# A two-layer graph network on one core: layer 1's decaying weights by byte additions in runs of eight nodes instead of by matmuls over every block

## The chip, the cores and the metric

The kernel runs on one core of a Trainium2 chip. The metric is the device time of one launch in microseconds. Before the change it was 696.75 us, the median of three runs (694.16, 696.75 and 701.30). A profile of one execution shows the engines: PE (TensorE matmuls, with PEld for its weight loads), DVE (VectorE), ACT (ScalarE), POOL (GpSimd), SP (SyncE, which here only issues transfers), and the queues of transfers (DMA).

## What is computed

There are 4096 nodes with 64 features, and a 0/1 adjacency matrix of 4096 x 4096 with about 8 ones in a row (67 MB in float32, the one large input).

```
h = relu(layernorm(x))
# layer 0: a weighted mean over the neighbours of a hyperbolic distance direction
w = adj / max(rowsum(adj), 1e-8)
agg = einsum('ij,ijc->ic', w, logmap(h_i, h_j))
x = x + expmap(0, agg @ W0 + b0)
h = relu(layernorm(x))
# layer 1: neighbours weighted by powers of a half, by their rank in the row
support = h @ W1
rank = cumsum(adj != 0, axis=1);  deg = rank[:, -1];  k = min(deg, 100)
w = (adj != 0) * where(rank - (deg - k) > 0, 0.5 ** (deg - rank), 0)
x = x + w @ support + b1
```

So in layer 1 the last neighbour of a row weighs 1, the one before it 1/2, and so on. In the kernel every degree is at most 30, else a second, dense path (not executed here) takes over.

## The kernel before

**Load.** The adjacency is read in 32 blocks of 128 rows. One call `load(rb, n)` (L789) issues two transfers of 256 KB on SP's queue into two of four buffers `a_sb`, transposes eight 128 x 128 pieces on PE against the identity (L799, the adjacency piece is the stationary operand) into the PSUM tile `a_ps`, and copies them with one ACT instruction (L801) as fp8 into `masks[q]`: partitions are columns of the adjacency (neighbours), the free dimension holds the rows. There are 128 such calls; `pack` (L808) follows each with eight small matmuls that pack 16 columns into one number.

**Lists.** For every second row block DVE searches the packed words for the largest entries (`search`, L835) and turns them into indices of neighbours (`ell_lists`, L849: the first eight words of a row). What does not fit goes through `tail_split`, `tail_first` and `tail_second` into short lists per quadrant of eight row blocks.

**Layer 0, by gathers.** There are 16 units of two row blocks. POOL fetches the neighbours' rows of the table `tab_d` (260 bytes each) with one indirect transfer per list slot (`gather`, L987 to L1000): 320 in all, 16 to 22 in a unit, into one of two buffers `g`. For the units that have tail entries POOL also makes a one-hot `oh` (`tail_rows`, L1012), which PE transposes (L1017), ACT copies (L1019) and PE multiplies (L1023, result `sel`). Then come `differ` (L1036 to L1058: DVE differences, ACT square), `weigh` (L1070 to L1089: from L1070 on, the buffer `g` is free again) and `total` (L1100 to L1119). When a group of row blocks has all its units, `middle` (L1144) makes layer 0's output, the layernorm and layer 1's `support`, which `split` (L1202) writes as three bf16 parts `sup`; it borrows two of the `a_sb` buffers.

**Layer 1, the powers.** `ranks(p, n, j)` (L1215) goes through the 32 column blocks j from the last to the first, for each of 4 quadrants p of 1024 rows and its two halves n of 512. A running tile `t` in PSUM counts the neighbours behind each column: one matmul with `rest` adds what block j+1 still lacked (L1221), one with `before` (lower triangular, with -128 on the diagonal) gives block j (L1225); then one ACT instruction writes 2^-(t) as fp8 over the mask, one block higher (L1229), so that a column without an edge becomes zero. PE and ACT take turns here: each step of PE needs the ACT result of the step before. That is 504 matmuls and 256 ACT instructions.

**Layer 1, the sum.** `collect(c, p, n)` (L1238) multiplies those weights with `sup` for four groups of column blocks `sums` (16, 8, 6 and 2 blocks), 1024 matmuls (L1244), and adds the three parts to `acc` on DVE (L1252, L1256): 64 such pairs. `write` stores `acc`.

**Order.** Every call gets a due time in `plan` by hand (`at`, L1267), and a scheduler at build time lays out one fixed order for every engine from these. At run time each engine goes through its own order and waits where an operand is late. So an instruction of `differ` can sit on PE, ACT or DVE behind a `load`, `ranks` or `collect` that comes first in that engine's order. SP's order is: x, 32 transfers of the adjacency, `tab_d` (L760), 12 more, `hp_d` (L767), and then the rest with the lists' small transfers in between.

Of the kernel before, what the change touches and what calls it, by code (L numbers as in the profile page):

```python
# [11 lines left out]
F32 = mybir.dt.float32  # L12
BF16 = mybir.dt.bfloat16
# [6 lines left out]
P = 128  # L20
# [19 lines left out]
BIG = 128.0  # L40
# [4 lines left out]
F8W = mybir.dt.float8e5  # L45

# [5 lines left out]
EXTRA = 8  # L52
TAILW = CAND - ELL + EXTRA
# [6 lines left out]
W8_SHIFT = 15  # L60
# [478 lines left out]
def kernel(  # L539
# [33 lines left out]
    UC = 512  # L573
    NU = N // UC
# [6 lines left out]
    x_v = x.rearrange("(b p) c -> p b c", p=P)  # L581
    out_v = out.rearrange("(b p) c -> p b c", p=P)
# [8 lines left out]
    def by_rows(t):  # L591
        return t.rearrange("(b p) c -> p b c", p=P)

    with ExitStack() as fast:
# [5 lines left out]
        ident = const.tile([P, P], F32, name="ident")  # L600
# [7 lines left out]
        w_c = const.tile([P, 1], F32, name="w_c")  # L608
        nc.vector.memset(w_c, (W8_SHIFT - BIG) * LN2)
# [11 lines left out]
        rest = const.tile([P, P], BF16, name="rest_b")  # L621
# [4 lines left out]
        nc.vector.tensor_scalar(grp_i, part_i, 4, None, ALU.logical_shift_right)  # L626
# [7 lines left out]
        nc.vector.tensor_scalar(pw_i, part_i, GRP - 1, None, ALU.bitwise_and)  # L634
        nc.vector.tensor_scalar(pw_i, pw_i, 135, None, ALU.add)
# [81 lines left out]
        masks = [maskp.tile([P, NB + 1, QR], F8, name=f"mask{q}") for q in range(NQ)]  # L717

        adjp = fast.enter_context(tc.tile_pool(name="adjp", bufs=4))
        lst = fast.enter_context(tc.tile_pool(name="lst", bufs=1))  # L720

        prep = fast.enter_context(tc.tile_pool(name="prep", bufs=1))
        late2 = masks[NQ - 2].bitcast(F32).rearrange("p b c -> p (b c)")[:, 16 * QR // 4 :]
        gn_i = late2[0:1, 0:NG].bitcast(I32)
        nc.gpsimd.iota(gn_i, pattern=[[1, NG]], base=0, channel_multiplier=0)
# [6 lines left out]
        nc.vector.scalar_tensor_tensor(tri_f, ident, -BIG, tri_f, ALU.mult, ALU.add)  # L732
        nc.vector.tensor_copy(before, tri_f)
        nc.vector.tensor_scalar(rest, tri_f, -1.0, 1.0, ALU.mult, ALU.add)
# [7 lines left out]
        nc.sync.dma_start(out=xin, in_=x_v)  # L742
        tab = part(NB * D, DT)
        sq = part(NB * (D + DT), D)
        x2 = prep.tile([P, NB], F32, name="x2")
        ab = prep.tile([P, NB], F32, name="ab")
        sg = prep.tile([P, NB], F32, name="sg")
        h = tab[:, :, 1:DT]
        layernorm_relu(prep, xin, h, sq)
# [23 lines left out]
        mid = fast.enter_context(tc.tile_pool(name="mid", bufs=1))  # L773
        ps_a = fast.enter_context(tc.tile_pool(name="ps_a", bufs=2, space=PSUM))
        ps_w = fast.enter_context(tc.tile_pool(name="ps_w", bufs=1, space=PSUM))
        ps_t = fast.enter_context(tc.tile_pool(name="ps_t", bufs=2, space=PSUM))
# [9 lines left out]
        sums = [(0, 16, (0, 1)), (16, 8, (2,)), (24, 6, (3,)), (30, 2, (4,))]  # L786


        def load(rb, n):  # L789

            a_ps = ps_a.tile([P, 2, SB, P], BF16, name="a_ps")
            for m in range(2):
                a_sb = adjp.tile([P, UC], F32, name="a_sb")
                c = 2 * n + m
                nc.sync.dma_start(out=a_sb, in_=adj[bass.ts(rb, P), bass.ts(c, UC)])

                upper = a_sb.bitcast(BF16)[:, 1 : 2 * UC : 2]
                for k in range(SB):
                    nc.tensor.transpose(a_ps[:, m, k, :], upper[:, bass.ts(k, P)], ident_b)  # L799
            q, b = divmod(rb, QB)  # L800
            nc.scalar.activation(  # L801
                masks[q][:, 2 * SB * n : 2 * SB * n + 2 * SB, bass.ts(b, P)],
                a_ps.rearrange("p m k f -> p (m k) f"),
                AF.Copy,
                saturate=False,
            )

        def pack(rb, n):  # L808
# [12 lines left out]
            for j in range(2 * SB * n, 2 * SB * n + 2 * SB):  # L821
                nc.tensor.matmul(  # L822
                    words[:, rb % 2, bass.ts(j, GB)],
                    lhsT=masks[q][:, j, bass.ts(b, P)],
                    rhs=pk,
                    start=False,
                    stop=True,
                    skip_group_check=True,
                )
# [19 lines left out]
        def ell_lists(rb, nb):  # L849
# [9 lines left out]
            nc.vector.tensor_scalar(  # L859
                ci, ci, NG - 1, 4, ALU.bitwise_and, ALU.logical_shift_left  # L860
            )
            nc.vector.tensor_scalar(e, w.bitcast(I32), 23, None, ALU.logical_shift_right)
            nc.vector.tensor_scalar(kk, e, -134.0, None, ALU.add)
            nc.vector.tensor_tensor(t, kk, ci, ALU.add)
            nc.vector.scalar_tensor_tensor(ell_v[:, r2], kk, 0.0, t, ALU.is_gt, ALU.mult)
            nc.vector.tensor_scalar(ell_i[:, r2], ell_v[:, r2], -1.0, 0.0, ALU.add, ALU.max)

        def tail_split(q):
# [12 lines left out]
            nc.vector.tensor_scalar(  # L881
                gf, gf, NG - 1, 4, ALU.bitwise_and, ALU.logical_shift_left
            )
            kk = e.bitcast(F32)
            t = p.bitcast(F32)
            for n in range(3):
# [5 lines left out]
                nc.vector.tensor_scalar(kk, e, -134.0, None, ALU.add)  # L892
                nc.vector.tensor_tensor(t, kk, gf, ALU.add)
# [5 lines left out]
                    ALU.is_gt,  # L899
# [244 lines left out]
        def middle(m, stage):  # L1144
# [5 lines left out]
            if stage == 0:  # L1150
                st["hq", m], st["xq", m] = (
                    adjp.tile([P, UC], F32, name="a_sb") for _ in range(2)
                )
            ht = st["hq", m][0:D, :]
            hq, xq = (
                st[k, m][:, 0 : nb * D].rearrange("p (b c) -> p b c", b=nb)
                for k in ("hq", "xq")
            )
            if stage == 0:
                nc.sync.dma_start(out=hq, in_=by_rows(tab_d)[:, bs, 1:DT])  # L1160
                nc.sync.dma_start(out=xq, in_=x_v[:, bs, :])
# [34 lines left out]
            else:  # L1196
                c = [m in s[2] for s in sums].index(True)
                if m == sums[c][2][0]:
                    st["sup", c] = blk.tile([P, sums[c][1], 3 * D], BF16, name=f"sup{c % 2}")
                sup = st["sup", c][:, b0 - sums[c][0] : b0 - sums[c][0] + nb, :]  # L1200

                def split(gs, sp):  # L1202
                    res = xq[:, gs, :]
                    rest = sp
                    for n in range(3):
                        part = sup[:, gs, n * D : n * D + D]
                        nc.vector.tensor_copy(part, rest)
                        if n < 2:
                            nc.vector.tensor_tensor(res, rest, part, ALU.subtract)
                        rest = res  # L1210

                product(m, v, w1_sb, ht, split)


        def ranks(p, n, j):  # L1215

            if j == NB - 1:
                st["t", p, n] = ps_t.tile([P, SW], F32, name="t")
            t = st["t", p, n]
            if j < NB - 1:  # L1220
                nc.tensor.matmul(  # L1221
                    t, lhsT=rest, rhs=masks[p][:, j + 1, bass.ts(n, SW)],
                    start=False, stop=False, skip_group_check=True,
                )
            nc.tensor.matmul(  # L1225
                t, lhsT=before, rhs=masks[p][:, j, bass.ts(n, SW)],
                start=(j == NB - 1), stop=True, skip_group_check=True,
            )
            nc.scalar.activation(  # L1229
                masks[p].bitcast(F8W)[:, j + 1, bass.ts(n, SW)],  # L1230
                t,
                AF.Exp,
                bias=w_c,
                scale=-LN2,
                saturate=False,
            )

        def collect(c, p, n):  # L1238

            b0, nb, _ = sums[c]  # L1240
            o = ps_a.tile([P, 2, 3 * D], F32, name="a_ps")
            for k in range(2):
                for j in range(nb):
# [151 lines left out]
```

## Time and profile before

| What | Value |
|---|---|
| median of three runs | 696.75 us |
| the profiled execution, first to last instruction | 888.9 us (its time outside that span isn't given) |
| first indirect transfer of POOL starts | 57.60 us |
| last POOL instruction ends | 813.1 us |
| transfers | 89.19 MB, 85,590 packets, 46,098 of them under 512 B |
| adjacency loads by the chain of waits | 22% of the span |
| TensorE clock granted, mean | 0.719 of full speed |

The profiled execution is 28% longer than the median run. All durations below come from it. Its table of groups gives, for each line and engine, how often an instruction ran, the mean duration, and how long the engine stood idle just ahead of it; its chain of waits follows the last instruction back to what released it; its table of windows gives the busy time of the engines in a stretch.

### The profile page before, as it was taken

The numbers are of one execution on the slowest core, as the hardware profiler recorded it, in microseconds if no ns is written. First come the engines' busy times: TensorE is split into PE (matmuls) and PEld (weight loads), VectorE is DVE, ScalarE is ACT, GpSimd is POOL, SyncE is SP. The second block draws the span as 40 slices with busy tenths as digits, with TensorE's granted clock in tenths as the row PEclk, the third lists the DMA queues.
The fourth block names the chain that finished last, engine by engine and source line by source line (L and its number), as shares of the span: only waits on it lengthen the run. The fifth ranks groups of instructions, "written<-read, shape, count | busy, mean of one in ns | idle before, by whom it ended". The sixth has DMA issues, their size and how long they took to land.

```text
span 888.9 us, 11822 instructions
## 1 busy us (share of the span) xinstructions
PE 494.8 (56%) x4170; PEld 328.1 (37%) x4170; DVE 411.1 (46%) x1482; ACT 356.6 (40%) x550; POOL 368.3 (41%) x396
## 2 busy tenths in 40 slices
PE   3654245277115656725727828576568574367495
PEld 2421123144002423513415403323258473267383
DVE  4550144266101637305624638604644244739786
ACT  3543246286115745815907828365511011202100
POOL 0035752603771046172172262736574818751000
PEclk9995576677556957966956968869559595569585
DMA  7899446386235756735836510301121101210002
GB/s 212 238 165 145 92 136 168 94 245 196 49 71 154 218 133 159 233 76 166 265 67 190 146 24 18 49 12 31 23 46 18 24 16 24 31 23 4 0 2 51
DMA packets 85590, 89.19 MB, mean 100 GB/s; under 512 B 46098, under 2 KB 47634, under 8 KB 85522
## 3 DMA queue, kind: packets, MB, share of 16 engines
q1 hardware_dynamic: 66194, 74.93, 31.2%
q0 software_dynamic: 10240, 10.67, 9.2%
q10 hardware_dynamic: 9088, 2.75, 1.5%
q8 instruction: 34, 0.56, 0.3%
q14 instruction: 34, 0.28, 0.1%
HBM read 84.12 MB, written 4.19 MB: 99 GB/s over the span
## 4 chain that ended last, share of the span: by engine, by line
PE 27%; DMA 24%; issue 14%; DVE 13%; another core or an unknown queue 11%; POOL 5%; ACT 4%; SPq 1%; ACTq 0%; DVEq 0%; POOLq 0%
DMA a_sb<-in_adj 22%; PE a_ps L1244 7%; PE a_ps L799 6%; POOL g L995 4%; PE t L1225 4%; PE t L1221 4%; DVE red L1252 2%; ACT mask L1229 2%; PE sel L1105 2%; DVE d L1070 2%; PE words L1139 1%; PE words L822 1%; DMA mask<-in_x 1%; DVE acc L1256 1%
## 5 line engine op out<-in xcount | busy, mean ns | idle before, releaser
L995 POOL DMA_INDIRECT g<-tab_d,ell_i x256 | 257.4, 1005 | 368.5 <-DVE u L1071 102.0
L1229 ACT ACTIVATE mask<-t,w_c 128x512 fp8e5<-128x512 f32 x256 | 172.3, 691 | 149.5 <-remote 65.2
L799 PE MATMUL a_ps<-ident_b,a_sb 128*128 128x128 bf16 x1024 | 128.6, 263 | 120.6 <-DMA a_sb<-in_adj 91.0
L801 ACT ACTIVATE mask<-a_ps 128x1024 fp8e4<-128x1024 bf16 x128 | 131.4, 1027 | 135.5 <-remote 78.8
L1221 PE MATMUL t<-mask,rest_b 128*128 128x512 fp8e4 x248 | 115.6, 466 | 78.8 <-ACT mask L1229 51.1
L799 PEld LDWEIGHTS <-a_sb 128*128 128x128 bf16 x1024 | 80.5, 116 | 189.5 <-DMA a_sb<-in_adj 130.2
L1225 PE MATMUL t<-mask,before 128*128 128x512 fp8e4 x256 | 121.7, 476 | 4.6 <-ACT mask L1229 4.6
L1244 PE MATMUL a_ps<-sup,mask 128*128 128x192 bf16 x1024 | 110.0, 271 | 24.1 <-issue 12.5
L1244 PEld LDWEIGHTS <-mask 128*128 128x128 fp8e5 x1024 | 98.0, 108 | 34.0 <-issue 29.4
L822 PE MATMUL words<-pk,mask 128*128 128x8 bf16 x1024 | 48.4, 170 | 67.7 <-ACT mask L801 34.6
L822 PEld LDWEIGHTS <-mask 128*128 128x128 fp8e4 x1024 | 44.4, 104 | 105.3 <-issue 56.4
L843 DVE MAX8 cand<-wsb 128x8 f32<-128x256 f32 x96 | 36.0, 411 | 86.2 <-ACT wsb L833 66.5
L1012 POOL TENSOR_SCALAR oh<-row,tail_r 128x128 bf16<-128x128 bf16 x64 | 46.9, 747 | 56.8 <-DVE r L1111 33.1
L995 POOL DMA_INDIRECT g<-tab_d,tail_i x64 | 62.2, 972 | 18.8 <-issue 18.8
L1225 PEld LDWEIGHTS <-before 128*128 128x128 bf16 x256 | 28.0, 110 | 109.2 <-issue 106.9
L1252 DVE TENSOR_REDUCE red<-a_ps 128x128 f32<-128x384 f32 x64 | 35.6, 556 | 51.0 <-remote 26.4
L1019 ACT COPY mt<-mi 128x768 bf16<-128x768 bf16 (+1 forms) x12 | 8.7, 728 | 93.4 <-PE mi L1017 93.4
L1221 PEld LDWEIGHTS <-rest_b 128*128 128x128 bf16 x248 | 28.8, 116 | 20.3 <-issue 11.8
L1139 PE MATMUL words<-w_sb,a_sb 64*128 64x64 f32 x128 | 26.4, 366 | 13.2 <-issue 7.6
L1036 DVE TENSOR_TENSOR d<-g,hi 128x1024 f32<-128x1024 f32 x16 | 19.4, 1215 | 28.6 <-DMA a_sb<-in_adj 28.4
L1105 PE MATMUL sel<-d,mr 128*128 128x65 f32 x128 | 24.0, 346 | 14.5 <-DVE r L1111 6.2
L1070 DVE TENSOR_REDUCE d<-g 128x22 f32<-128x1408 f32 (+2 forms) x16 | 23.7, 1482 | 17.8 <-ACT g L1058 9.6
(285 smaller groups left out, 555.0 us busy)
## 6 DMA issues: line engine op xcount, KB each, us to landing
a_sb<-in_adj SPq DMA_DIRECT2D x256, 256.0 KB
g<-tab_d,ell_i POOLq DMA_INDIRECT x256
hp_d<-mask SPq DMA_DIRECT2D x1, 1560.0 KB
hr<-hp_d ACTq DMA_DIRECT2D x8, 146.2 KB
tab_d<-mask SPq DMA_DIRECT2D x1, 1040.0 KB
hi<-tab_d ACTq DMA_DIRECT2D x16, 64.0 KB
g<-tab_d,tail_i POOLq DMA_INDIRECT x64
out<-acc SPq DMA_DIRECT2D x8, 128.0 KB
```

Of the source, the lines that this page charges most:

```text
L799: nc.tensor.transpose(a_ps[:, m, k, :], upper[:, bass.ts(k, P)], ident_b)
L801: nc.scalar.activation(masks[q][:, 2 * SB * n : 2 * SB * n + 2 * SB, bass.ts(b, P)], a_ps.rearrange("p m k f -> p (m k) f"), AF.Copy, satu ...
L822: nc.tensor.matmul(words[:, rb % 2, bass.ts(j, GB)], lhsT=masks[q][:, j, bass.ts(b, P)], rhs=pk, start=False, stop=True, skip_group_check= ...
L995: nc.gpsimd.indirect_dma_start(out=g[:, k, :], out_offset=None, in_=tab_d, in_offset=bass.IndirectOffsetOnAxis(ap=i, axis=0),)
L1012: nc.gpsimd.tensor_scalar(oh[:, k, :], row128, row[:, k : k + 1], None, ALU.is_equal)
L1070: nc.vector.tensor_reduce(d2, u["g"][:, 0:ns, 1:DT], AX.X, ALU.add)
L1105: nc.tensor.matmul(ag[:, k // TB, :], lhsT=mr[:, k, :], rhs=d[:, E2 + k, :], start=(k % TB == 0), stop=(k % TB == TB - 1),)
L1221: nc.tensor.matmul(t, lhsT=rest, rhs=masks[p][:, j + 1, bass.ts(n, SW)], start=False, stop=False, skip_group_check=True,)
L1225: nc.tensor.matmul(t, lhsT=before, rhs=masks[p][:, j, bass.ts(n, SW)], start=(j == NB - 1), stop=True, skip_group_check=True,)
L1229: nc.scalar.activation(masks[p].bitcast(F8W)[:, j + 1, bass.ts(n, SW)], t, AF.Exp, bias=w_c, scale=-LN2, saturate=False,)
L1244: nc.tensor.matmul(o[:, k, :], lhsT=masks[p].bitcast(F8W)[:, b0 + j + 1, bass.ts(2 * n + k, P)], rhs=st["sup", c][:, j, :], start=(j == 0) ...
L1252: nc.vector.tensor_reduce(red, o.rearrange("p k (n c) -> p k c n", n=3), AX.X, ALU.add)
```

## The change

Nodes are renumbered: a partition now holds runs of eight neighbouring nodes (node = 1024 s + 8 p + l, with s a group of 1024 nodes, p the partition, l the place in the run) in place of nodes p apart by 128. So the eight column blocks of one s hold, on each partition, a run of eight consecutive columns. The transfers of x, of the table, of `hp_d` and of the output become contiguous per partition, and a load takes 1024 columns in one transfer of 512 KB, with three buffers of 4 KB per partition in place of four of 2 KB. The transposes read the adjacency with a stride of 32 bytes in place of 4.

The mask is stored as fp8 2^-14, whose byte is 4. `suffix(p, s)` adds bytes two at a time as int16 on DVE, so that each column of a run holds four times the count of edges at and behind it in the run; ACT then copies the run's total. `ranks(p, s)` counts over runs only, with `upto` and `before` (14 matmuls per quadrant in place of 126), ACT turns the result into a base byte per run, and one DVE instruction subtracts the eight columns' bytes from it. The byte is then read as fp8: its exponent is the power of two. As every column now has a value, edge or not, the sum over edges is done by parts: `middle` makes differences of `support` of neighbouring columns, over the runs with help of two small matmuls (`shift`, `carry`), and `collect` sums 33 blocks in five groups in place of 32 in four. `keep` copies `support` on ACT. The indices of the lists are made for the new numbers, with as many instructions.

In the built order POOL has the same 320 indirect transfers and 64 one-hots as before. `middle` takes one of the three `a_sb` buffers; in the built order of SP its first call now stands ahead of the last 22 of the 128 loads, where before all loads came first, and the searches of row blocks 24 to 31 stand on DVE behind units 8 and 9. The byte additions of a quadrant stand on DVE among the steps of `weigh`, `total` and `tail_split`.

```diff
-    x_v = x.rearrange("(b p) c -> p b c", p=P)
+    x_v = x.rearrange("(s p l) c -> p s l c", p=P, l=RUN)
+    adj_v = adj.rearrange("(s p l) c -> s l p c", p=P, l=RUN)
     def by_rows(t):
-        return t.rearrange("(b p) c -> p b c", p=P)
+        return t.rearrange("(p b) c -> p b c", p=P)
...
-        adjp = fast.enter_context(tc.tile_pool(name="adjp", bufs=4))
+        masks = [maskp.tile([P, NB, QR], F8W, name=f"mask{q}") for q in range(NQ)]
+        words16 = [m.bitcast(I16) for m in masks]
+        adjp = fast.enter_context(tc.tile_pool(name="adjp", bufs=3))
...
-        sums = [(0, 16, (0, 1)), (16, 8, (2,)), (24, 6, (3,)), (30, 2, (4,))]
+        sums = [range(0, 8), range(8, 16), range(16, 24), range(25, 30), (24, 30, 31, None)]
         def load(rb, n):
-            a_ps = ps_a.tile([P, 2, SB, P], BF16, name="a_ps")
-            for m in range(2):
-                a_sb = adjp.tile([P, UC], F32, name="a_sb")
-                c = 2 * n + m
-                nc.sync.dma_start(out=a_sb, in_=adj[bass.ts(rb, P), bass.ts(c, UC)])
...
+            a_sb = adjp.tile([P, UC], F32, name="a_sb")
+            nc.sync.dma_start(out=a_sb, in_=adj_v[rb // RUN, rb % RUN, :, bass.ts(n, UC)])
+            upper = a_sb.bitcast(BF16)[:, 1 : 2 * UC : 2].rearrange("p (f l) -> p l f", l=RUN)
+            a_ps = ps_a.tile([P, RUN, P], BF16, name="a_ps")
+            for l in range(RUN):
+                nc.tensor.transpose(a_ps[:, l, :], upper[:, l, :], ident_b)
...
+                def keep(gs, sp):
+                    nc.scalar.copy(v[:, gs, :], sp)
+                product(m, v, w1_sb, ht, keep)
...
+                    pv = ps_o.tile([P, SW], F32, name="o")[:, 0:D]
+                    nc.tensor.matmul(
+                        pv, lhsT=shift, rhs=st["y", s - 1][:, RUN - 1, 0:D], start=True, stop=(s == 1)
+                    )
...
+                    nc.vector.tensor_tensor(dd[:, 0, :], pv, v[:, 0, :], sub)
+                    nc.vector.tensor_tensor(dd[:, 1:n, :], v[:, 0 : n - 1, :], v[:, 1:n, :], sub)
...
+        def suffix(p, s):
+            w = words16[p][:, bass.ts(s, RUN), :]
+            for l in reversed(range(RUN - 1)):
+                nc.vector.tensor_tensor(w[:, l, :], w[:, l, :], w[:, l + 1, :], ALU.add)
+            tb = st["tb", p, s] = tbp.tile([P, QR], F8, name="tb")
+            nc.scalar.activation(
+                tb, masks[p].bitcast(U8)[:, s * RUN, :], AF.Copy, scale=1.0 / STEP, saturate=False
+            )
-        def ranks(p, n, j):
+        def ranks(p, s):
...
+            for n in range(2):
+                if s < NS - 1:
+                    nc.tensor.matmul(
+                        t[:, n, :], lhsT=upto, rhs=st["tb", p, s + 1][:, bass.ts(n, SW)],
+                        start=False, stop=False, skip_group_check=True,
+                    )
                 nc.tensor.matmul(
+                    t[:, n, :], lhsT=before, rhs=st["tb", p, s][:, bass.ts(n, SW)],
+                    start=(s == NS - 1), stop=True, skip_group_check=True,
                 )
+            base = mid.tile([P, QR], U8, name="base")
             nc.scalar.activation(
-                masks[p].bitcast(F8W)[:, j + 1, bass.ts(n, SW)],
-                t,
-                AF.Exp,
...
+                base, t.rearrange("p n c -> p (n c)"), AF.Identity, bias=top_c, scale=-STEP
+            )
+            w = words16[p][:, bass.ts(s, RUN), :]
+            nc.vector.tensor_tensor(
+                w, base.bitcast(I16).unsqueeze(1).to_broadcast([P, RUN, QR // 2]), w, ALU.subtract
             )
...
         for p in range(NQ):
-            for j in reversed(range(NB)):
-                for n in range(QR // SW):
-                    at(t, ranks, p, n, j)
-                    t += 1.0
-            made[p] = t + 2.0
+            for s in reversed(range(NS)):
+                at(t, suffix, p, s)
+                at(t + 4.0, ranks, p, s)
+                t += 8.0
+            made[p] = t + 6.0
```

## The prediction, made before the changed kernel ran

> **What bounds the kernel now.** I read the busy shares first, then the windows by stage, then who waits on POOL, then the stretches that these waits point to.
>
> ```profile
> PE 494.8 (56%) x4170; PEld 328.1 (37%) x4170; DVE 411.1 (46%) x1482; ACT 356.6 (40%) x550; POOL 368.3 (41%) x396
> ```
>
> No engine is full, so the order of waits decides. POOL's work is one long row: 320 indirect transfers that run at a fixed pace. Its first starts at 57.60 us and its last instruction ends at 813.1 us. The windows that end where POOL's second half begins (504.5) and where it ends:
>
> ```profile
> 0.00:504.50 504.50, 254.59 (x2504) 153.87 (x2505) 195.23 (x760) 249.79 (x346) 190.49 (x206) 0.73 0.63 159
> 504.50:813.50 309.00, 194.35 (x1329) 136.48 (x1329) 160.38 (x527) 97.71 (x180) 177.82 (x190) 0.72 0.17 25
> 813.50:888.90 75.40, 45.90 (x342) 37.75 (x339) 55.53 (x198) 9.11 (x26) 0.00 (x0) 0.66 0.07 16
> ```
>
> The columns are PE, PEld, DVE, ACT, POOL, granted clock, DMA share, GB/s. The adjacency comes in up to 504; PE and ACT are each half busy there. Afterwards transfers hardly matter (25 GB/s), POOL works to 813, and a tail of 75 us on DVE and PE follows.
>
> ```profile
> POOL g L995 <- DVE u L1071: 102.0, 6, 23.3
> POOL g L995 <- issue: 91.0, 302, 0.3
> POOL g L995 <- DVE d L1070: 60.4, 3, 39.3
> POOL g L995 <- DMA tab_d<-mask: 55.1, 1, 55.1
> POOL g L995 <- ACT mask L1229: 45.7, 2, 37.7
> POOL oh L1012 <- DVE r L1111: 33.1, 3, 17.6
> ```
>
> The 91.0 us of "issue" are a fixed 0.30 between transfers, so one costs 0.945 + 0.30 = 1.25 us. POOL's work between 57.6 and 813.1 is 319.6 + 91.0 + 46.9 (one-hots) = 457.5 us of 755.5. The other 298 us are stalls, mostly for a free buffer `g` (L1070, L1071): 207 ahead of 504.7 (447 long, 170.3 + 51 + 18.4 = 240 of work), and 91 behind.
>
> Why a buffer comes free late is seen in one unit (columns: start, duration):
>
> ```profile
> 581.68 2.35 POOL L1012 TENSOR_SCALAR oh<-row,tail_r 128x128 bf16<-128x128 bf16 x4
> 595.79 0.22 PE L1017 MATMUL mi<-ident_b,oh 128*128 128x128 bf16 x1
> 599.16 0.42 DVE L1051 TENSOR_TENSOR d<-g,sel 128x256 f32<-128x256 f32 x1 [21.06 <-PE sel L1023]
> 601.18 1.49 DVE L1070 TENSOR_REDUCE d<-g 128x20 f32<-128x1280 f32 x1 [0.91 <-ACT g L1058]
> ```
>
> The one-hot was ready at 584.0, but PE transposed it only at 595.8: in PE's order `ranks` steps stand ahead, each in turn with ACT. POOL stood still from 586.5 to 602.9.
>
> **Profile and median.** The span is 888.9, the median 696.75, 192 less. In the chain of waits up to 504 us, 149 us are "issue" or an unknown queue, and 70 behind, together 219: time in which nothing that the profile shows was awaited. I take the 192 out of POOL's stalls, some 140 in the first part and 50 in the second. The median is then about 57.6 + 457.5 + 106 of stalls + 75.8 = 697; this split is an estimate.
>
> **The change part by part.**
>
> *Start.* `tab_d` is issued at 40.30 and POOL's first transfer comes 17.3 later. The transfer moves 1.04 MB in 4096 pieces of 260 bytes; in runs of 8320 bytes, at the 212 to 238 GB/s of the first two slices, 4.7 us. It still stands behind as many bytes of adjacency (18 transfers of 512 KB for 32 of 256) and the lists of row blocks 0 and 1 were ready at 37. So -12 us; bounds 0 (the loads ahead go slower) and -17 (it costs nothing).
>
> *Matmuls of the ranks.* 504 are removed and 56 added: 448 x 0.471 (the mean of L1221 and L1225) = 211 us of PE. On ACT 256 x 0.691 (L1229, 172.3 in its row of groups) go; 16 copies of 1024 elements at 1.03 (L801) and 16 of twice L1229's width (at most 1.38) come, 39 in all, so -134. Neither lies on POOL, so it counts only through the stalls. In the first part ACT loses most of 134 of some 250 us, so `load`, `weigh` and the lists' copies follow each other sooner. In the example 12 of 16.5 us of a stall were PE's queue of ranks. But `collect` still stands in the same places behind 650, where stalls of 6.4, 9.5, 16.8 and 17.6 us occur that no ranks caused. I take just under half of the 106 us: -50. Bounds: 0 (the next late thing is as late) and -90 (POOL hardly stalls).
>
> *Byte additions on DVE.* 112 of 128x512 and 16 over 4096 elements, all with two inputs. The trace has no two-input row with 16-bit data throughout. Dearest: the float32 rows, 0.685 (L1171, 512 elements) and 1.118 ns an element (L766, 2.326 us for 2080): 112 x 0.685 + 16 x 4.58 = 150 us. Cheapest: the cast at 1.245 for 2080 elements (L764), 0.60 ns: 112 x 0.31 + 16 x 2.45 = 74. I take 150, since two inputs are nearer in kind than a cast. DVE then has some 561 us of work in about 655, so it isn't full, and much of it fits where it waited (it was busy 195 of 504). The Trainium skill ("VectorE: DVE Perf Modes", The perf-mode tier table) says that a two-input operation doubles its rate with 16-bit data in SBUF; by it the sum would be 74, and no run here shows it.
>
> What the additions do cost is POOL's pace. A transfer of POOL that meets a two-input instruction of DVE gets longer:
>
> ```profile
> 56.74 2.33 DVE L766 TENSOR_TENSOR mask<-mask,mask 128x2080 f32<-128x2080 f32 x1 [4.91 <-DMA tab_d<-mask]
> 57.60 2.87 POOL L995 DMA_INDIRECT g<-tab_d,ell_i  x1 [55.10 <-DMA tab_d<-mask]
> 60.38 2.33 DVE L766 TENSOR_TENSOR mask<-mask,mask 128x2080 f32<-128x2080 f32 x1
> 60.77 3.33 POOL L995 DMA_INDIRECT g<-tab_d,ell_i  x1 [0.30 <-issue]
> ```
>
> 2.87 and 3.33 in place of 0.945: 4.3 us lost in about 7.2 us of DVE, 0.6. Over the whole trace 46 transfers took over 1.0 us, 17.2 us too long in sum, beside some 127 us of longer two-input work in POOL's stretch: 0.13. At 0.12 (POOL is more often at work then, but not all will meet): 150 x 0.12 = +18 us. Bounds: 74 x 0.1 = 7 and 150 x 0.6 = 90.
>
> *Loads.* The same 1024 transposes, 128 copies, 1024 packings. Half the transfers, twice the size; in flight up to 1.5 MB for 1.0. Already in the sum of stalls: nothing more. The stationary reads stride 32 bytes. Rows: 116 ns at a stride of 4 bytes (L799), 104 dense (L822). If a step eight times as long cost as much again, 1024 x 0.116 = 119 us of PE would come in the first part, in the room that the ranks leave (211); I take 0, bound +15. The Trainium skill ("SBUF — State Buffer", Door 1: The DMA port swizzle, its note on cachelines) speaks against this: an access that leaves a line of 16 bytes pays. It gives no price for weight loads, and no row here has such a stride.
>
> *Sum by parts.* 32 matmuls more (32 x 0.271 = 9 us of PE), 16 more pairs of L1252 and L1256, 16 x 0.846 = 13.5 us of DVE. Behind POOL's end 40 pairs are left in the built order for 32: 8 x 0.846 = 7 us. Sums begin with one group of 8 in place of two, which takes work out of the tail. +2 us net, bounds -10 and +12.
>
> *Late loads.* 22 loads stand behind the first `middle`: 11.5 MB, 52 us at 220 GB/s. On DVE the last lists stand some 2.5 units of 31 us (78 us) behind it: hidden, 0; if not, up to 50 of POOL.
>
> Sum: 697 - 12 - 50 + 18 + 2 = 655 us.
>
> **Rivals.**
> *Byte additions hold POOL* (slower). Place: DVE bursts of about 37 us per quadrant, back to back as at 57 to 64 us, where the loss was 0.6. Price 150 x 0.6 = 90: 697 - 12 - 50 + 90 + 2 = 727. It decides once the hold passes 62 us, 0.41 per us. For it: those two rows. Against: the mean of 0.13, and additions are spread among other steps.
> *The gathers' own chain sets the pace* (no gain from ranks). One-hot, transposes, square and L1070 stay in series and loads or `collect` stand where ranks stood: 697 - 12 + 18 + 2 = 705.
> *POOL all but full.* 697 - 12 - 90 + 7 = 602. For it: 134 and 211 us gone from ACT and PE. Against: the stalls behind 650.
> *Late lists.* 655 + 50 = 705, if the last 22 loads run at half rate.
>
> **How the numbers follow.** Forecast (620 to 688) 0.55, POOL full 0.12, own chain 0.13, late lists 0.05, additions hold POOL 0.15. About 1% (7 us) is what a measurement of this kernel can tell from no change. Faster: 0.55 + 0.12 = 0.67, and 0.02 of the two at 705 fall there. Within 1%: 0.07 of those two. Slower: 0.15 + their last 0.09. The range takes in POOL full and the two at 705, and stops short of 727: 600 to 714.
>
> **What would show it.** POOL's first transfer near 45 us if the start is right. L1171-like widths in the byte rows of 0.69 us (or about 0.3) settle their price; the mean of the indirect transfers, 0.999 now, would be 1.05 for the forecast and near 1.28 for the first rival. POOL's stalls in the page should fall by 50 or more, above all those put down to ACT and PE. A wait of `cand` or of POOL for the last loads would show late lists. If POOL's stalls are as long as before though PE and ACT are idle, my step from freed engines to freed buffers is wrong.

## The result, and the profile after

The changed kernel takes 711.80 us (median of four runs, 711.52 to 713.68), beside 695.45 us for the kernel before (median of four): a ratio of 1.028, with a 95% interval of 1.022 to 1.034. It is slower, where 655 was forecast. The time lies just inside the stated range (600 to 714).

The profile shown before the prediction (span 888.9 us) and the first four runs below were taken where the kernel before takes about 870 us, which happened on one of the five chips whose number is recorded, so these times are compared only with each other; on the other four chips, and in the profile after (span 709.8 us), it does not occur.

The page's busy times and the three groups of instructions that carry the result (busy us and mean ns of one, then the idle time ahead):

```profile
PE 384.3 (54%) x3768; PEld 317.1 (45%) x3768; DVE 483.8 (68%) x1635; ACT 238.7 (34%) x335; POOL 409.8 (58%) x396
...
L1014 POOL DMA_INDIRECT g<-tab_d,ell_i x256 | 298.1, 1164 | 190.8 <-issue 71.6
...
L1258 DVE TENSOR_TENSOR mask<-mask 128x512 int16<-128x512 int16 x112 | 42.7, 414 | 15.1 <-PE words L845 14.8
...
L1284 DVE TENSOR_TENSOR mask<-base,mask 128x4096 int16<-128x4096 int16 x16 | 36.5, 2279 | 7.4 <-ACT base L1280 7.4
```

Against the kernel before, as profiled at a span of 699.7 us (PE 482.7, ACT 355.1, POOL 367.7), PE lost 98 us of busy time and ACT 116. The byte steps cost DVE 42.7 + 36.5 = 79 us. POOL's own busy time rose from 368 to 410 us with the same 396 instructions: its indirect transfers became longer, 1.164 us in the mean for those of the lists.

Who waits on POOL, in the changed kernel:

```profile
POOL g L1014 <- issue: 89.7, 298, 0.3
POOL g L1014 <- DVE kk L884: 42.5, 1, 42.5
POOL g L1014 <- DVE d L1089: 30.4, 4, 12.4
POOL g L1014 <- DVE u L1090: 24.1, 4, 14.4
POOL oh L1031 <- DVE r L1130: 11.6, 1, 11.6
POOL g L1014 <- DVE tl L934: 10.8, 1, 10.8
POOL g L1014 <- DVE scr L912: 7.1, 1, 7.1
```

42.5 is the start. Every stall over 2 us that follows it is put down to DVE; none to PE or ACT any more. Between 45 and 300 us DVE is busy 187.2 of 255 us in the changed kernel and 136.6 in the kernel before (both from the profiles of 710 and 700 us used below; columns as in the prediction's windows, DVE is the third busy time):

```profile
45.00:300.00 255.00, 136.86 (x1488) 106.28 (x1488) 187.21 (x667) 128.09 (x153) 169.75 (x145) 0.67 0.68 210
45.00:300.00 255.00, 179.91 (x1761) 108.87 (x1762) 136.57 (x541) 177.93 (x254) 162.25 (x165) 0.78 0.84 221
```

Two stretches of the timeline show two ways in which the byte steps reach POOL (columns: start, duration, engine). First, transfers beside subtractions:

```profile
125.81 0.95 POOL L1014 DMA_INDIRECT g<-tab_d,ell_i  x1 [0.30 <-issue]
...
127.62 2.28 DVE L1284 TENSOR_TENSOR mask<-base,mask 128x4096 int16<-128x4096 int16 x1
128.43 2.29 POOL L1014 DMA_INDIRECT g<-tab_d,ell_i  x1 [0.30 <-issue]
131.03 0.94 POOL L1014 DMA_INDIRECT g<-tab_d,ell_i  x1 [0.30 <-issue]
131.88 2.28 DVE L1284 TENSOR_TENSOR mask<-base,mask 128x4096 int16<-128x4096 int16 x1
132.27 2.73 POOL L1014 DMA_INDIRECT g<-tab_d,ell_i  x1 [0.30 <-issue]
135.31 0.95 POOL L1014 DMA_INDIRECT g<-tab_d,ell_i  x1 [0.30 <-issue]
```

These two transfers, each beside a subtraction, take 2.3 and 2.7 us in place of 0.945. Second, the longest stall of the row, 280.3 to 294.7:

```profile
276.76 3.51 POOL L1031 TENSOR_SCALAR oh<-row,tail_r 128x128 bf16<-128x128 bf16 x6
...
284.88 2.29 DVE L1284 TENSOR_TENSOR mask<-base,mask 128x4096 int16<-128x4096 int16 x1 [7.38 <-ACT base L1280]
...
288.63 1.22 DVE L1055 TENSOR_TENSOR d<-g,hi 128x1024 f32<-128x1024 f32 x1
...
292.80 1.60 DVE L1089 TENSOR_REDUCE d<-g 128x22 f32<-128x1408 f32 x1
...
294.47 0.19 DVE L1090 TENSOR_TENSOR u<-rj,d 128x22 f32<-128x22 f32 x1
...
294.68 1.03 POOL L1014 DMA_INDIRECT g<-tab_d,ell_i  x1 [14.40 <-DVE u L1090]
```

DVE stood still for 7.38 us in front of a subtraction whose base byte ACT had not made. 4.6 of these fall into POOL's stall of 14.4, so that part of it is not DVE's work, but a wait that the subtraction brought into DVE's order. Behind it in DVE's order were the search and list steps and the unit's `differ` and `weigh` (L1055 to L1090), which free POOL's buffer.

### The profile page after: what moved, and what is told of

The parts are those of the page before. It is cut to its first block, busy times and chain, and to the rows that moved or that the text cites. A ratio compares the mean times of both kernels' runs of the same rounds, so it can differ in the third digit from the quotient of the medians.

```text
span 709.8 us, 10724 instructions
## 1 busy us (share of the span) xinstructions
PE 384.3 (54%) x3768; PEld 317.1 (45%) x3768; DVE 483.8 (68%) x1635; ACT 238.7 (34%) x335; POOL 409.8 (58%) x396
## 4 chain that ended last, share of the span: by engine, by line
POOL 38%; DVE 20%; DMA 14%; PE 12%; issue 12%; ACT 2%; SPq 1%; DVEq 0%; ACTq 0%; POOLq 0%
POOL g L1014 33%; DMA a_sb<-in_adj 8%; PE a_ps L1296 6%; POOL oh L1031 5%; DVE red L1304 3%; DMA g<-tab_d,ell_i 3%; PE a_ps L821 3%; DVE mask L1284 2%; DVE d L1089 2%; PE words L1158 1%; DVE acc L1308 1%; DVE d L1055 1%; DMA g<-tab_d,tail_i 1%; DVE d L1134 1%; PE sel L1042 1%
## 5 line engine op out<-in xcount | busy, mean ns | idle before, releaser
L1014 POOL DMA_INDIRECT g<-tab_d,ell_i x256 | 298.1, 1164 | 190.8 <-issue 71.6
L823 ACT ACTIVATE mask<-a_ps 128x1024 fp8e5<-128x1024 bf16 x128 | 129.6, 1024 | 123.6 <-PE a_ps L821 123.1
L821 PEld LDWEIGHTS <-a_sb 128*128 128x128 bf16 x1024 | 101.4, 162 | 78.6 <-DMA a_sb<-in_adj 76.7
L1296 PEld LDWEIGHTS <-mask 128*128 128x128 fp8e5 x1024 | 95.6, 106 | 20.8 <-issue 18.0
L1014 POOL DMA_INDIRECT g<-tab_d,tail_i x64 | 70.3, 1098 | 18.4 <-issue 18.1
L845 PEld LDWEIGHTS <-mask 128*128 128x128 fp8e5 x1024 | 43.7, 108 | 41.5 <-ACT mask L823 29.8
L1036 PE MATMUL mi<-ident_b,oh 128*128 128x128 bf16 x64 | 16.4, 279 | 84.2 <-POOL oh L1031 83.9
L1258 DVE TENSOR_TENSOR mask<-mask 128x512 int16<-128x512 int16 x112 | 42.7, 414 | 15.1 <-PE words L845 14.8
L1124 PEld LDWEIGHTS sel<-d,mr 128*128 128x128 f32 x128 | 24.3, 286 | 48.4 <-issue 44.5
L1284 DVE TENSOR_TENSOR mask<-base,mask 128x4096 int16<-128x4096 int16 x16 | 36.5, 2279 | 7.4 <-ACT base L1280 7.4
L1154 PE MATMUL o<-ext,y 128*64 128x128 f32 x64 | 15.6, 384 | 40.4 <-DVE y L696 19.6
L1077 ACT ACTIVATE g<-d 128x1408 f32<-128x1408 f32 (+2 forms) x16 | 20.3, 1271 | 38.0 <-DVE w L1073 10.1
```

The costliest lines, as they stand in the source:

```text
L821: nc.tensor.transpose(a_ps[:, l, :], upper[:, l, :], ident_b)
L823: nc.scalar.activation(masks[q][:, bass.ts(n, RUN), bass.ts(b, P)], a_ps, AF.Copy, scale=2.0**-ONE_SHIFT, saturate=False,)
L845: nc.tensor.matmul(words[:, rb % 2, bass.ts(j, GB)], lhsT=masks[q][:, j, bass.ts(b, P)], rhs=pk, start=False, stop=True, skip_group_check= ...
L1014: nc.gpsimd.indirect_dma_start(out=g[:, k, :], out_offset=None, in_=tab_d, in_offset=bass.IndirectOffsetOnAxis(ap=i, axis=0),)
L1124: nc.tensor.matmul(ag[:, k // TB, :], lhsT=mr[:, k, :], rhs=d[:, E2 + k, :], start=(k % TB == 0), stop=(k % TB == TB - 1),)
L1258: nc.vector.tensor_tensor(w[:, l, :], w[:, l, :], w[:, l + 1, :], ALU.add)
```

## The experiments

Theory A: two-input byte instructions of DVE hold POOL's transfers. Theory B: DVE's time in the fixed order delays what frees POOL's buffers. Theory C: the 22 loads behind the first `middle` delay the lists. Three numbers of POOL's row are worked out from its timeline for every run: its first transfer; the *excess*, the sum over 320 transfers of what each took above 0.945 us; and the *stalls*, the sum of what lies between its instructions above 0.30 us, from the first transfer on.

### First runs, where the kernel before takes 869.5 us

The kernel before, unchanged:

> The kernel before, unchanged, for a profile whose span is nearer to its median: the profiled execution of before was 888.9 us long, the median 695. If my split of the median holds (start 57, POOL's work 457, stalls 106, tail 76), the profile shows a span near 695 with POOL's first transfer near 57, its mean near 1.0 us and stalls over 0.3 us of about 106 in sum. If the kernel before had less stall than I took, there was less to gain: stalls of 60 to 80, and more time elsewhere.

878.25 us; stalls 279 us, excess 18.7. The long times are not made by profiling: seven timed runs beside it take 861.95 to 878.26. The chain of waits puts 18% of the span down to "another core or an unknown queue", which the profile after does not show.

`e1_no_byte_steps` leaves the byte steps out (so the powers are not formed):

```diff
-            for l in reversed(range(RUN - 1)):
-                nc.vector.tensor_tensor(w[:, l, :], w[:, l, :], w[:, l + 1, :], ALU.add)
...
-            nc.vector.tensor_tensor(
-                w, base.bitcast(I16).unsqueeze(1).to_broadcast([P, RUN, QR // 2]), w, ALU.subtract
-            )
+            nc.vector.tensor_copy(w[:, 0, 0:1], base.bitcast(I16)[:, 0:1])
```

> The changed kernel without the 112 byte additions and with the 16 subtractions cut to one element; the weights are then the bare marks, so layer 1's sum is another one, everything else is done. Theory A (these two-input instructions hold POOL's transfers): the mean of an indirect transfer falls from 1.15 to about 1.05 us, 320 x 0.09 = 28 us off POOL's work, time 680 to 685. Theory B (they cost DVE its time, and buffers come late): stalls of POOL fall instead, by up to the 84 us there are; time 650 to 690 with the mean of a transfer still near 1.15. Theory C (late loads and order, not bytes): 705 to 712.

`e2_one_input_instead` puts one-input reductions of about the same time in their place (bytes not added):

```diff
+                f = w.bitcast(BF16)
+                nc.vector.tensor_reduce(f[:, l, 0:1], f[:, l, 0:256], AX.X, ALU.max)
...
+            nc.vector.tensor_reduce(f[:, 0, 0:1], f[:, 0:4, :], AX.XY, ALU.max)
```

> The changed kernel with each byte addition replaced by a reduction of about the same length that has one input (256 elements in place of 512, near 0.41 us; 2048 in place of the 4096 of the subtraction, near 2.28 us). DVE keeps its time, its order and its waits; only the second input is gone. It leaves the counting of ranks out. Theory A: as fast as the kernel without byte steps, 680 to 685, transfers near 1.05 us. Theory B: as slow as the changed kernel, 708 to 714, though transfers get shorter.

`e3_loads_first` makes `middle` due after the loads, as before the change:

```diff
-                at(z + z0, middle, m, k % 4)
-                ready[m] = z + z0 + 3.0
+                zm = max(z, TLOADED + 4.0 + 12.0 * m)
+                at(zm + z0, middle, m, k % 4)
+                ready[m] = zm + z0 + 3.0
```

> The changed kernel with the due times of middle as in the kernel before (not ahead of the end of the loads), so that in the built order all 128 loads come before the first middle takes a buffer. Theory C (late loads hold up the last lists, and with them POOL): 15 to 30 us less, 682 to 697. Theories A and B: 705 to 715, within 1% of the changed kernel, since POOL was at work when the late loads came.

792.0, 839.2 and 820.4 us: ratios of 0.916 (0.906 to 0.926), 0.969 (0.961 to 0.977) and 0.944 (0.933 to 0.954). All three lie below the kernel before, e3 too, which leaves nothing out; but the runs there scatter by up to 2%, so they are a hint and no more. The changed kernel was not run in this condition, so its parts can't be priced here, and the runs were repeated beside it elsewhere.

### Beside the changed kernel, where the kernel before takes 695 us

> The changed kernel unchanged, beside the kernel before on the same chip. Two theories of why it is slower. A: the byte additions of DVE hold POOL's indirect transfers (66 us above 0.945 in its own profile, 18 before). C: the order, 22 loads behind the first middle, makes POOL wait. Either gives 1.02 to 1.04 where the kernel before takes about 695 us. Where the kernel before takes about 870 us, as in the four runs before this, the change would come out faster: the run without byte steps took 792 us there, and 40 to 50 us of holds on top give 832 to 842, a ratio of 0.96 to 0.97.

> The 112 additions and 16 subtractions on bytes left out once more, now beside the changed kernel on the same chip. A: below the changed kernel by the whole excess of the transfers, 45 to 50 us, and the transfers' mean falls from 1.16 to about 1.03 us. C: below it by less than 15 us, because the late loads still stand behind the first middle.

> The changed kernel with middle due after the loads, as before the change. A: as the changed kernel, within 10 us, since the same additions hold the same transfers. C: 25 to 40 us below the changed kernel, because the gap in the loads from 260 to 378 us closes and POOL's waits for the last lists go.

`h1_table_only` is the kernel before with the contiguous table alone:

```diff
-        return t.rearrange("(b p) c -> p b c", p=P)
+        return t.rearrange("(p b) c -> p b c", p=P)
...
-        nc.vector.tensor_scalar(grp_i, part_i, 4, None, ALU.logical_shift_right)
+        nc.vector.tensor_scalar(grp_i, part_i, GB - 1, None, ALU.bitwise_and)
...
+            pattern=[[1, NB], [NB, GB]], base=0, channel_multiplier=0,
...
-            nc.vector.tensor_scalar(kk, e, -134.0, None, ALU.add)
+            nc.vector.tensor_scalar(kk, e, -135.0, float(NG), ALU.add, ALU.mult)
```

> The kernel before with one part of the change: the table and its neighbours in DRAM contiguous per partition (node p + 128 b at row 32 p + b), the lists' indices made for it; ranks, loads and sum as before. The start is 10 to 13 us earlier by both theories (first indirect transfer near 45 us). If POOL's row of transfers sets the end, the time falls by those 10 to 13 us; if the loads set when the last lists come, by less than 5.

The kernel before here: 695.24. The changed kernel 711.67 (1.026; 1.022 to 1.031); without byte steps 650.00 (0.938; 0.933 to 0.942); loads first 718.40 (1.034; 1.029 to 1.039); the table alone 673.50 (0.970; 0.966 to 0.974), **faster than both kernels**, with nothing left out. So the byte steps cost 62 us, more than the 45 to 50 that A named, and C falls: with the loads first it is no faster. The granted TensorE clock, which is lower in the changed kernel (0.63 to 0.69 in its runs, 0.80 to 0.81 in those of the kernel before), doesn't explain the loss: without the byte steps it is 0.63 to 0.70, at 650 us.

### What in the byte steps costs

> The kernel before unchanged, for a profile where it takes about 695 us (the one shown before the prediction had a span of 888.9). If that profile differs from this one only by longer stalls of POOL, as the prediction assumed, POOL's first transfer comes at 57 us, its stalls over 0.3 us between instructions add up to about 106, its excess of transfers over 0.945 us is below 20 and 76 us follow its end. If it was a condition of its own, the excess may be about 28, as with the table alone changed, and the stalls below 100.

> The byte additions and subtractions replaced by one-input reductions of about the same DVE time (the bytes are then not added). A (two-input instructions hold POOL's transfers): excess of the transfers near 30 us as without byte steps, and a time some 35 us below the changed kernel, 670 to 680. B (DVE's time and its fixed order are what costs): as the changed kernel, 705 to 715.

`e5_no_subtraction` leaves out the second half of the edit of e1 alone:

> Only the 16 subtractions over 4096 elements left out (one element copied instead); the 112 additions stay. They are 36.5 of the 79 us of byte steps on DVE. A: excess of the transfers down from 65 to some 45 us, by the 20 that overlap with them in the profile of the changed kernel, and 25 to 40 us less in all. If the many small additions are what costs, less than 15 us.

`e7_slow_form` (the subtraction is written in the same way):

```diff
-                nc.vector.tensor_tensor(w[:, l, :], w[:, l, :], w[:, l + 1, :], ALU.add)
+                nc.vector.scalar_tensor_tensor(
+                    w[:, l, :], w[:, l, :], 1.0, w[:, l + 1, :], ALU.mult, ALU.add
+                )
```

> The same additions and subtractions, same result, written as scalar-tensor-tensor (times 1.0, then add or subtract) in place of tensor-tensor. If that form does not get the doubled rate, the 79 us of DVE become about 130. A, hold by any two-input instruction for as long as it runs: excess of the transfers rises from 65 to about 85 to 95 us and the time to 740 to 765. A2, hold only by the doubled-rate form: excess falls to about 30 us and the time is 690 to 720 (35 less hold, more DVE).

Later, with the same medians of before (695.65 and 697.10): `e8_one_input_writes`,

```diff
+                f = w.bitcast(BF16)[:, l, 0:256]
+                nc.vector.tensor_reduce(f, f.unsqueeze(2), AX.X, ALU.max)
...
+            f = w.bitcast(BF16)[:, 0:4, :]
+            nc.vector.tensor_reduce(f, f.unsqueeze(3), AX.X, ALU.max)
```

> As the run with one-input reductions, but each reduction is over an axis of length 1, so it writes as many elements as it reads (256 and 2048, bf16), in the same built order on SP, and about the same DVE time. If full-width writing is what holds POOL's transfers, their excess rises from 28 us to 55 to 65 and the time from 700 to 725 to 740. If the second input is what holds, excess stays at 26 to 32 us and the time at 693 to 707.

`h3_table_no_ranks`, h1 with an empty `ranks` and `collect` reading the raw mask:

> The kernel with the table alone changed (673.5 us), with the matmuls and the exponentials of the ranks left out (the sum then takes the raw mask). This prices freeing PE and ACT by itself, without byte steps. The prediction took 50 us for it: 623. The run of the changed kernel without byte steps stood 24 us below the table alone: if that was the ranks' share, 642 to 655; if the changed kernel's loads and sum by parts cost time of their own there, below 635.

`e10_split_subtraction`:

```diff
+            for l in range(RUN):
+                nc.vector.tensor_tensor(w[:, l, :], base.bitcast(I16), w[:, l, :], ALU.subtract)
```

> Each subtraction over 4096 elements is written as eight of 512, same result; DVE time of the subtractions rises from 36.5 to about 53 us. Leaving out the subtractions took 23 us of excess for 36.5 us of DVE (0.64 per us), leaving out the additions another 12 for 42 us (0.28). If long instructions hold more per us than short ones, excess falls from 65 to 52 to 60 us and the time stays within 10 us of 711. If it goes by DVE time alone at about 0.45 per us, excess rises to 70 to 76 and the time to 720 to 735.

and `e11_one_input_same_order`, where each reduction also reads the next column, as the additions do (the subtractions are replaced as in e8):

```diff
+                nc.vector.tensor_reduce(
+                    f[:, l, 0:256].rearrange("p (a b) -> p a b", a=2),
+                    f[:, l : l + 2, 0:128].unsqueeze(3), AX.X, ALU.max,
+                )
```

> The one-input reductions again, written as wide as they read and with the same chain from column to column as the additions, so that the order built on SP is that of the changed kernel almost word for word (18 loads ahead of the table, where the two earlier one-input runs had 24 and a start 11 us later). DVE time as in the changed kernel. What remains above the run without byte steps (650) is DVE's time in the fixed order, what is missing to the changed kernel (711.7) is the hold by the second input. Hold worth its excess: 670 to 680, first transfer near 45 us, excess 25 to 30 us, stalls 75 to 90. DVE's time worth as much as in the earlier run: 690 to 697, stalls about 105.

All runs where the kernel before takes 694 to 697 us (us; the last column is what follows POOL's last instruction in the profiled span):

| Run | Median (profiled span) | First transfer | Excess | Stalls | Behind POOL |
|---|---|---|---|---|---|
| before, again | 701.5, one run (699.7) | 56.4 | 23.9 | 106.2 | 76.3 |
| table alone | 673.5 (676.2) | 47.7 | 28.1 | 89.0 | 73.7 |
| table alone, no ranks | 652.8 (652.1) | 48.6 | 26.8 | 66.2 | 73.9 |
| change, no byte steps | 650.0 (647.3) | 44.9 | 29.8 | 60.3 | 75.7 |
| change, no subtractions | 681.5 (683.4) | 46.1 | 41.5 | 82.6 | 75.1 |
| change, one input, same order | 695.8 (689.8) | 45.8 | 28.6 | 102.7 | 75.2 |
| change, one input, wide writes | 704.2 (700.8) | 56.9 | 25.0 | 106.7 | 75.9 |
| change, one input, narrow writes | 699.9 (700.2) | 56.5 | 28.3 | 103.2 | 75.1 |
| **change** | 711.7 (709.7) | 45.6 | 64.7 | 84.5 | 78.0 |
| change, subtraction in eight | 708.1 (706.2) | 44.8 | 60.3 | 84.2 | 78.7 |
| change, loads first | 718.4 (719.6) | 44.8 | 66.9 | 94.7 | 75.7 |
| change, slow form | 787.6 (785.7) | 45.5 | 113.8 | 110.6 | 78.3 |

*The hold is real, and reductions with one input don't cause it.* In the run of the changed kernel, 24 transfers overlap a subtraction; they took 28.8 us too long in 30.9 us of overlap (2.14 us each in the mean, in place of 0.945). In the slow form (4.41 us a subtraction) it was 55.6 in 54.9. With one-input reductions of 2.27 us, which write all they read, they took 1.7 us too long in 18.1:

```profile
118.62 2.27 DVE L1290 TENSOR_REDUCE mask<-mask 128x2048 bf16<-128x2048 bf16 x1
118.90 0.94 POOL L1014 DMA_INDIRECT g<-tab_d,ell_i  x1 [0.30 <-issue]
120.15 0.94 POOL L1014 DMA_INDIRECT g<-tab_d,ell_i  x1 [0.30 <-issue]
...
123.87 2.27 DVE L1290 TENSOR_REDUCE mask<-mask 128x2048 bf16<-128x2048 bf16 x1
123.89 0.94 POOL L1014 DMA_INDIRECT g<-tab_d,ell_i  x1 [0.30 <-issue]
```

This is e11, of the one-input runs the one whose order is nearest to the changed kernel's. Wide or narrow writes made no difference to the excess (25.0 and 28.3), and the form without the doubled rate held as much per us, so neither the writing nor the doubled rate is the cause. The second input is what the two holding forms share. But a reduction differs from a subtraction in its operation and type too (bf16 for int16), and one input alone is no safe sign: in the changed kernel's own profile, a cast with one input held a transfer for 0.61 us in 0.74 us of overlap, with nothing of size beside it but a maximum search (in the slow form's run, two transfers beside nothing but such searches lost nothing in 1.2 us):

```profile
47.88 1.29 DVE L788 CAST mask<-mask 128x2080 bf16<-128x2080 f32 x1
...
48.43 1.56 POOL L1014 DMA_INDIRECT g<-tab_d,ell_i  x1 [0.30 <-issue]
...
49.09 0.73 DVE L866 MAX8 cand<-wsb 128x8 f32<-128x256 f32 x2
```

*But the hold is the smaller share of the time.* With nearly the changed kernel's order and DVE time but without the hold (e11), the time is 695.8: 16 us below the change (19 by the ratios, 0.998 to 1.026, as the two ran on different chips), though the excess fell by 36. The other part came back as stalls, 102.7 for 84.5. Its waits say for whom:

```profile
POOL g L1014 <- DVE d L1089: 48.2, 6, 13.9
POOL g L1014 <- DVE kk L884: 43.5, 2, 43.2
POOL oh L1031 <- DVE r L1130: 13.0, 1, 13.0
POOL g L1014 <- DVE scr L913: 12.3, 1, 12.3
POOL g L1014 <- DVE ta L952: 11.8, 1, 11.8
```

43.2 of the second row is the start. POOL comes sooner and waits longer for the same DVE. Against the run without byte steps (650.0) that is 46 us (42 by the ratios) for 78 us of DVE work and its waits: theory B. In the POOL stalls of more than 1.3 us, DVE was at work for 45 of 62 us without byte steps and for 84 of 104 in e11, so the longer stalls are mostly DVE's work. So of the 62 us, about 46 are DVE's time in its order, and the hold adds 16 on top.

One rival to the 46 was left open. The scheduler lays the order out anew for every kernel: apart from the byte steps, DVE's instructions stand a median of 10 places elsewhere without byte steps than in the changed kernel (of 1507; at most 112), but 1 place in e11 (at most 37). So the 16 compare nearly the same order, while the 46 hold what the other order is worth, too; no run parts the two.

The two earlier one-input runs were muddied: as their reductions don't depend on each other, the build put 28 of them ahead of the table's last step on DVE, and 24 loads in place of 18 ahead of the table on SP, so POOL began 11 us later. Without the subtractions the time fell by 30 us (36.5 us of DVE), the additions took the other 31 (42.7 us): nearly in proportion to DVE's time, though the excess is 23 and 12. The slow form came out beyond both of its expectations (740 to 765, or 690 to 720): with 64 us more of DVE and 49 more of excess it took 76 us more. In eight pieces the subtraction cost 10 us more of DVE and 4 us less of excess; the ratios, 1.018 (1.014 to 1.022) and 1.026 (1.022 to 1.031), just touch, and whether length matters by itself stays open.

## Why the prediction was wrong

The steps as priced, and as the runs showed them one after another (before 695.2 to 695.7, table 673.5, ranks out 652.8, the rest of the change without byte steps 650.0, the change 711.7):

| Step | Taken | Measured |
|---|---|---|
| start (table contiguous) | -12 | -22 |
| ranks off PE and ACT | -50 | -21 |
| loads, sum by parts, late loads | +2 | -3 |
| byte additions | +18 | +62 |
| sum | -42 | +16 |

The 56 matmuls and 32 ACT instructions of the new ranks, which the prediction counted against the second row, stand in the third row's -3.

**Profile and median: right, as far as one run shows.** The split into 57.6 + 457.5 + 106 + 75.8 = 697 was an estimate; the kernel before, profiled at 699.7 us, has its first transfer at 56.4, stalls of 106.2 and 76.3 behind POOL.

**Start: right in kind, too small.** The first transfer came 8.8 us earlier with the table alone; another 17 us came out of the stalls. Why they shrink was not tested apart.

**Ranks: the second term that failed, by its size.** 504 matmuls and 256 exponentials out of the way shortened the stalls from 89.0 to 66.2. "Just under half of the 106" was a guess from one stall, and the term measured less than half of it: what was next late was DVE, to which all but 10 us of the stalls that were left there are put down. The work taken off PE was overstated too: the two rows of groups of the ranks add up to 227 us in the run with the table alone, but PE's busy time fell only from 466.1 to 383.9 when they went; records of PE overlap, and the other matmuls took longer (transposes 307 ns in the mean for 259).

**Byte additions: the step that failed.** The term said that DVE "isn't full, and much of it fits where it waited (it was busy 195 of 504)", and so priced DVE's time at nothing and only the hold. Two errors partly cancelled inside the term and one did not: the DVE time was half of what was taken (79 for 150 us, from rows of 414 and 2279 ns); the hold per us was not 0.12 but (64.7 - 28.6) / 79 = 0.46, near the first rival's 0.6; and DVE's own time, costed at zero, was worth about 46, with the reservation made above on the order. The Trainium skill's rule ("VectorE: DVE Perf Modes", The perf-mode tier table) that a two-input operation doubles its rate with 16-bit data would have given 74, an estimate that the 79 bear out. The two transfers from which the prediction read 0.6 us per us each overlapped a cast as well as a two-input subtraction, and the cast holds, too (0.61 us in 0.74). The trace of before had that sign: the waits on POOL already named DVE at L1070, L1071 and L1111 for 195 us. An engine that POOL waits for is not slack because its mean share is below half: between 45 and 300 us it was busy 54% before and 73% after (65% without the byte steps, so not all of that is theirs), and in DVE's order byte steps stand ahead of the units' steps, as in the stretch at 284 us.

**Rivals.** The first, "byte additions hold POOL" (727), had the right place and nearly the right rate of hold; it was dearer than what came because it took 150 us of DVE, and its mechanism alone explains 16 of the 62 (19 by the ratios). The second, "the gathers' own chain sets the pace" (705), came nearest in time, with the wrong reason: the ranks did give something, and DVE took it back. "Late lists" fell with the loads-first run, and "POOL all but full" (602) with the runs without ranks and without byte steps, in which POOL still stalled for 66 and 60 us. That 711.8 lies inside the range is luck: its upper end was set for the two rivals at 705, whose reasons did not hold.

**Weight loads with a stride of 32 bytes** went from 116 to 162 ns in the mean, 21 us of busy time in all (80.5 to 101.4), within the 119 taken as the most. The Trainium skill's note on cachelines ("SBUF — State Buffer", Door 1: The DMA port swizzle) points the same way and gives no price. It costs nothing that can be seen in the time: the whole rest of the change, beside the table, the old ranks and the byte steps, is worth -3 us.

The signs named for the start held (45.07 us). The mean of the transfers, 1.15 us over both kinds, fell between the forecast's 1.05 and the first rival's 1.28. POOL's stalls should have fallen by 50 or more; they fell by 22 (106.2 to 84.5), and those put down to PE and ACT went, as said, while DVE kept POOL waiting.

## What to carry to other kernels

Work that is moved to an engine has to be priced by who waits for that engine, not by its mean busy share: here 78 us on a DVE that was 59% busy cost about 46 us, and nearly all of the stalls in the row that sets the end are waits for DVE. Before an accelerator of one engine's work is traded for work on another, each part of the change is worth trying alone: the contiguous table by itself is 3% faster than the kernel before, and was lost inside a change that is 3% slower. And when a hold is measured as excess over a fixed pace, it must be compared with a run in which the hold alone is gone: about half of these 36 us were time that POOL would have waited in any case.

## What the runs showed of the hardware

The byte instructions of DVE with two inputs in SBUF held an indirect transfer issued by POOL: 0.93 us per us of overlap at 2.28 us a subtraction (16-bit, 2279 ns for 4096 elements), 1.0 at 4.41 us (the slower form), about 0.5 for additions of 0.41 us (14.9 us in 30.1), and next to nothing for one-input reductions of the same time (0.1). A one-input cast of float32 to bf16 held as well (0.61 us in 0.74). The Trainium skill ("SBUF — State Buffer", Who interferes with whom) says that a DVE instruction with two inputs in SBUF contends with a POOL instruction that reads SBUF, and that a reduction never does; both fit these runs, as an indirect transfer here reads its list (`ell_i`) from SBUF. The page also infers that the making of a transfer's descriptors is not stalled by tensor-tensor; these indirect transfers were held by it, and whether that was at the reading of the list or at the descriptors, no run here tells.

The scalar-tensor-tensor form takes 682 and 4410 ns where the tensor-tensor form takes 414 and 2279 on the same 16-bit data. And the same program took 695 us on four chips and 870 on a fifth, where its chain of waits shows 18% of the span under "another core or an unknown queue"; what that is, no run here tells.
